# A graph layer on one core: cold edge lists read tile by tile, hot lists read from both ends of a block

## The chip, the cores and the metric

The kernel runs on one core of one Trainium2 chip. The metric is the device time of one launch in microseconds. The profiled execution is one launch recorded by the hardware profiler. The engines are PE (TensorE), DVE (VectorE), ACT (ScalarE), POOL (GpSimd) and SP (SyncE); each runs its instructions in program order and waits for others by semaphores.

## The reference

There are 6250 nodes with 256 features, and 200000 edges from `src` to `dst`, sorted by `dst`. `src` is uniform; `dst` is 6250 times the square of a uniform number, so that low node numbers are frequent destinations.

```python
xn = layernorm(x)
w  = sigmoid(relu(xn @ W1 + b1) @ W2 + b2)            # one number per node
num = segment_sum((xn * w)[dst], src); den = segment_sum(w[dst], src)
x = x + num / max(den, 1e-12) + mix(xn)                # mix: per-head linear attention over all nodes
f = layernorm(x)
# a router picks 2 of 6 experts; each expert is three 256x256 layers, the first two with relu
x = x + sum of the two experts' outputs, weighted
```

The part that the change touches is the pair of segment sums: for each node, the sum over its edges of the row `[xn * w, w]` of the other end.

## The kernel before, in words

The nodes are cut into 49 tiles of 128 (the last has 106), two tiles make a block of 256 (25 blocks), four tiles a group. A node's row `[xn * w, w, 1]` of 258 numbers is written to DRAM (`y_rows`) as three bf16 terms whose sum is the fp32 value, 774 numbers in all.

The edges are split by their place in the list, which is sorted by `dst`. Edges 0 to 65535 are the hot piece `b`: their destinations lie in the first 6 tiles. Edges 65536 to 131071 and 131072 to 196607 are the cold pieces `a` and `c`. The last 3392 are "few" edges; they are gathered 128 at a time (L501) and added to a table in DRAM by a scattering DMA (L522).

**Sorting.** Each piece is sorted on the chip by source node (`sort`, a bitonic network on DVE with turns on PE and copies back by ACT, L304 and L305), and written to DRAM as a list of packed keys (L346). `counts` finds where each block begins in a list: for each block border, one ACT activation (L354) takes the sign of `src` minus the border over the piece's 65536 edges and sums it; a matmul with ones adds the partitions, and `starts_of` turns the sums into `starts`.

**Cold edges.** For each block, `window_load` reads from each cold list a window of 23 x 128 keys that begins at the block's start. `cold_window` turns it and splits the keys into `dsts` and `srcs`. A cold step handles 128 edges: POOL gathers their 128 rows from `y_rows` by an indirect DMA (L851), DVE builds a 0/1 matrix `hot1` of edge against node (L859), and PE multiplies that matrix with the three terms of the gathered rows into the tile's sum `pu` (L876, three matmuls). The keys are in order of source, so the first tile of a block uses columns 0 to 11 of a window and the second columns 9 to 22; columns 9 to 11 hold edges of either, are gathered once and used in two steps. A block with both pieces has 52 steps and 46 gathers. Gathered rows lie in `GBUF` = 22 buffers. For the first 4 blocks (`LEAD`) piece `a` is done alone, then `c`, as `c` is sorted later. `Cold.step` is written so that gathers and matrices are issued `AHEAD` = 10 steps before their matmuls.

**Hot edges.** For each block a window of 23 x 128 keys is read from list `b`. In it the edges are in order of destination. `hot_counts` builds for each column `j` a matrix `to` (edge against source in the block, L1020) and, for each of 6 destination tiles `d` and each column that can hold edges into `d`, a matrix `fr` (edge against destination, L1022); their product, summed over columns (L1029), is a table of counts that is then multiplied with the hot rows, which stay in SBUF (L1048). `hot_range(blk, d)` gives the columns: the expected place of `d`'s edges, five standard deviations wide on both sides.

**The order of the work.** It is written out by a planner while the program is built. `run` interleaves generators (`Line`) by costs and due times that they yield; the first stretch interleaves the deviations of the first layernorm, the node rows (`node_rows`, `lines_y`), the sort of `a`, and the counts of `a` (`line_u[0]`). In the second, cold steps are paced by due times and run beside the few edges, the other two sorts and the head products; ACT's loads of the expert weights (L917 and after) reuse memory that the few edges' tiles held. From the first node term (L1073) on, class `Work` spends a credit after each cold step on node terms, hot sums and expert matmuls (L1188 bias, L1201, L1218). The credit per step is

```python
credit += max(0.0, (work.left - LAST) / (len(steps_c) - cold_edges.done + 1))
```

so that the cold steps spread evenly over the rest of the work, with `LAST` left for after the last of them. `ALL` is the planner's estimate of all that work. At the end the kernel sums the numbers of edges it has counted, and does all edges again by a slow path if the sum isn't 200000.

The functions as they stand before the change:

Of the kernel before, what the change touches and what calls it, by code (L numbers as in the profile page):

```python
# [27 lines left out]
GBUF = 22  # L28
# [10 lines left out]
class Piece:  # L39
# [4 lines left out]

    def __init__(self, name, start, row, used, cap, first, second):
        self.name, self.start, self.row, self.used, self.n = name, start, row, used, row * P
        self.cap, self.first, self.second = cap, first, second
# [3 lines left out]
def kernel(  # L51
# [61 lines left out]
    cold = [Piece("a", 65536, 512, P, 23, 12, 9), Piece("c", 131072, 512, P, 23, 12, 9)]  # L113
    hot = Piece("b", 0, 512, P, 23, 23, 0)
    pieces = cold + [hot]
    FEW = 196608
    NFEW = -(-(E - FEW) // P)
    HOT = 6
    NTHR = NBLK - 1
# [3 lines left out]
    def hot_range(blk, d):  # L123
        per = hot.n * min(BN, N - blk * BN) / N

        def bound(k, sign):
            at = min(1.0, E / hot.n * (P * k / N) ** 0.5) * per
            return at + sign * 5 * at**0.5

        lo = 0 if d == 0 else int(bound(d, -1) // P)  # L130
        hi = -int(-bound(d + 1, 1) // P)
        return max(0, lo), min(hot.cap, hi)
# [36 lines left out]
    nc.gpsimd.iota(thr, pattern=[[-BN, NTHR]], base=-BN, channel_multiplier=0, allow_small_or_imprecise_dtypes=True)  # L169
# [179 lines left out]
    def counts(i):  # L349

        p = pieces[i]
        junk = pool_of(p).tile([P, p.row], BF, name=f"junk_{p.name}")
        for b in range(NTHR):
            nc.scalar.activation(  # L354
                junk, raw[p.name][0], AF.Sign, bias=thr[:, b : b + 1], accum_out=cnts[:, i, b : b + 1]
            )
            yield 0, 60 + 1.1 * p.row

    starts = const.tile([P, len(pieces), NBLK], I32, name="starts")
    nc.vector.memset(starts, 0)  # L360

    def starts_of(i0):
# [394 lines left out]
    with tc.manual_schedule(engines=ORDERED):  # L757
# [4 lines left out]
        line_t.before = line_u[0].before = [line_l]  # L762
        first_lines = [line_l, line_d] + lines_y + [line_a, line_u[0], line_t]
# [17 lines left out]
    def window_keys(wt, name):  # L781
# [4 lines left out]
        keys = wn.tile([P, 2 * max(p.cap for p in pieces)], I32, name="keys")[:, :n]  # L786
# [3 lines left out]
    def cold_window(wt):  # L790

        keys, n = window_keys(wt, "a")
        dsts = wn.tile([P, 2 * cold[0].cap], I32, name="dsts")[:, :n]
        nc.vector.tensor_scalar(dsts, keys, (1 << LOW) - 1, None, op0=ALU.bitwise_and)
        srcs = wn.tile([P, 2 * cold[0].cap], I32, name="srcs")[:, :n]
# [9 lines left out]
    for i, (blk, ps) in enumerate(passes):  # L805
        first_step.append(len(steps_c))
        for half in range(min(SB, NTILE - blk * SB)):
            todo, c0 = [], 0
            for p in ps:
                a, b = (0, p.first) if half == 0 else (p.second, p.cap)  # L810
                todo += range(c0 + a, c0 + b)
                c0 += p.cap
            steps_c += [(i, half, j, j == todo[0], j == todo[-1]) for j in todo]

    class Cold:
# [9 lines left out]
        def load(self, i):  # L825

            while self.loaded <= min(i, len(passes) - 1):
# [3 lines left out]
                self.wt[self.loaded] = window_load(blk, ps, "a")  # L831
                self.loaded += 1

        def decode(self, i):
            self.load(i)
            dsts, srcs = cold_window(self.wt.pop(i))
            loc = wn.tile([P, 2 * cold[0].cap], FP, name="loc")[:, : srcs.shape[1]]
# [3 lines left out]
        def make(self):  # L841
# [7 lines left out]
            if (i, j) not in self.gts:  # L849
                gt = gp.tile([P, TERMS, W], BF, name="gt")  # L850
                nc.gpsimd.indirect_dma_start(  # L851
                    out=gt.rearrange("p k w -> p (k w)"),
                    out_offset=None,
                    in_=y_rows,
                    in_offset=bass.IndirectOffsetOnAxis(ap=dsts[:, j : j + 1], axis=0),
# [613 lines left out]
```

## Time and profile before

| | us |
|---|---|
| median of 3 runs | 2080.5 (2080.08 to 2090.24) |
| the profiled execution | 2081.42 |
| its span, first to last instruction | 2079.2 |

| engine | busy us | share | instructions |
|---|---|---|---|
| PE | 1800.9 | 87% | 10048 |
| DVE | 1328.0 | 64% | 5556 |
| ACT | 540.0 | 26% | 1100 |
| POOL | 1158.2 | 56% | 1195 |

How to read it: busy time counts an instruction from its start to its end, so that on POOL the time between two instructions is not counted, and PE's matmuls overlap, their ends being modelled. Shares of the whole span are averages over stages with different limits; the mean granted PE clock was 0.923 over the span and 1.00 from about 650 us on. The costliest groups of the page are the gathers (L851, x1128, 1083.3 us of POOL) and the cold matmuls (L876, x3816, which are 1272 steps of three).

### The profile page before, as it was taken

To read this page: it belongs to the slowest core of one execution; us is meant where nothing else is said; L and a number is where in the kernel's file an instruction comes from. 1 tells how busy PE (TensorE), PEld (TensorE's weight loads), DVE (VectorE), ACT (ScalarE), POOL (GpSimd) and SP (SyncE) were. 2 spreads that over 40 slices of the span, in tenths; PEclk is the share of its full clock that TensorE was granted. 3 is DMA by queue.
4 is the path that set the end of the run, shared out by engine and by line. 5 is a ranking of instruction groups with operands and counts; after the bars stand their busy time and mean duration, and the time that the engine had idled before them with its cause. 6 is when DMAs were issued, how large, how long until landed. Compare 5 with 4: busy or idle time off the path is not lost.

```text
span 2079.2 us, 31214 instructions
## 1 busy us (share of the span) xinstructions
PE 1800.9 (87%) x10048; PEld 1221.6 (59%) x10048; DVE 1328.0 (64%) x5556; ACT 540.0 (26%) x1100; POOL 1158.2 (56%) x1195
## 2 busy tenths in 40 slices
PE   0664499645588999999999999999999999999998
PEld 0343377423455676666766667666666666666556
DVE  8989778948786655557555656655656565565322
ACT  0675443100011212212121221212122122222332
POOL 0000267777556777676777767777776767760000
PEclk9765599867789999999999999999999999999999
DMA  9742356576546566565665656566565666650000
GB/s 256 233 152 83 88 136 163 126 203 192 151 128 174 150 165 182 148 185 149 174 178 155 194 144 177 163 163 189 159 182 157 164 180 164 194 140 18 1 11 14
DMA packets 158713, 311.04 MB, mean 150 GB/s; under 512 B 28859, under 2 KB 101728, under 8 KB 158544
## 3 DMA queue, kind: packets, MB, share of 16 engines
q0 software_dynamic: 77728, 232.33, 42.0%
q1 hardware_dynamic: 75460, 76.12, 11.7%
q10 hardware_dynamic: 5356, 0.55, 0.3%
q8 instruction: 80, 1.31, 0.3%
q14 instruction: 89, 0.73, 0.1%
HBM read 275.51 MB, written 33.40 MB: 149 GB/s over the span
## 4 chain that ended last, share of the span: by engine, by line
PE 69%; DVE 6%; DMA 1%; issue 1%; ACT 0%; DVEq 0%; SPq 0%; ACTq 0%
PE px L1201 24%; PE pu L876 18%; PE px L1218 12%; PE ph L1029 5%; PE ph L1048 5%; PE px L1188 1%; DVE fr L1022 1%; PE ph L1073 1%; PE px L1108 1%; DVE to L1020 1%; PE px L1101 0%; DVE hot L859 0%; PE px L1114 0%; DVE k_b L268 0%; DVE k_b L269 0%
## 5 line engine op out<-in xcount | busy, mean ns | idle before, releaser
L851 POOL DMA_INDIRECT gt<-y_rows,dsts x1128 | 1083.3, 960 | 675.4 <-DVE srcs L796 241.6
L876 PE MATMUL pu<-gt,hot 128*128 128x258 bf16 x3816 | 625.6, 282 | 3.6 <-DMA gt<-y_rows,dsts 3.0
L876 PEld LDWEIGHTS <-hot 128*128 128x128 bf16 x3816 | 381.7, 101 | 341.3 <-issue 258.6
L1022 DVE TENSOR_SCALAR fr<-count,rdl 128x128 bf16<-128x128 bf16 x1105 | 273.6, 270 | 95.8 <-PE ph L1029 94.9
L1210 ACT ACTIVATE h<-px,eb_t 128x512 f32<-128x512 f32 (+1 forms) x312 | 206.6, 662 | 429.2 <-PE px L1201 428.4
L859 DVE TENSOR_SCALAR hot<-count,loc 128x128 bf16<-128x128 bf16 x1272 | 292.3, 272 | 18.2 <-PE pu L876 17.2
L1201 PE MATMUL px<-fT,ew_t 128*128 128x512 f32 (+1 forms) x624 | 298.2, 573 | 0.3 <-ACT fT L1102 0.3
L1201 PE MATMUL px<-h,ew_t 128*128 128x512 f32 (+1 forms) x624 | 297.1, 570 | 0.0
L1218 PE MATMUL px<-ew_t,h 128*128 128x256 f32 (+1 forms) x1176 | 296.6, 380 | 0.0
L1227 DVE SCALAR_TENSOR_TENSOR acc<-px,gate,acc 128x256 f32<-128x256 f32 (+1 forms) x294 | 128.6, 478 | 196.6 <-PE px L1218 196.4
L1029 PE MATMUL ph<-to,fr 128*128 128x256 bf16 x1105 | 225.4, 280 | 19.6 <-DVE fr L1022 15.3
L1218 PEld LDWEIGHTS px<-ew_t,h 128*128 128x128 f32 (+1 forms) x1176 | 203.4, 190 | 25.0 <-issue 4.3
L1020 DVE TENSOR_SCALAR to<-count,hloc 128x256 bf16<-128x256 bf16 x562 | 170.5, 305 | 2.0 <-PE ph L1029 2.0
L1031 ACT CAST cn<-ph 128x256 bf16<-128x256 f32 x150 | 55.8, 372 | 361.4 <-PE ph L1029 355.5
L1029 PEld LDWEIGHTS <-fr 128*128 128x128 bf16 x1105 | 109.2, 99 | 65.9 <-DVE fr L1022 39.4
L1048 PE MATMUL ph<-yh,cn 128*128 128x258 bf16 x882 | 130.9, 273 | 0.0
L1058 DVE TENSOR_TENSOR cs<-ph,cs 128x258 f32<-128x258 f32 x49 | 20.9, 427 | 150.8 <-PE ph L1048 150.3
L1201 PEld LDWEIGHTS px<-fT,ew_t 128*128 128x128 f32 x624 | 96.3, 191 | 22.0 <-issue 14.9
L1201 PEld LDWEIGHTS px<-h,ew_t 128*128 128x128 f32 x624 | 95.8, 190 | 22.1 <-issue 17.6
L1048 PEld LDWEIGHTS <-cn 128*128 128x128 bf16 x882 | 85.7, 97 | 15.4 <-issue 2.3
L545 PE MATMUL turn<-ident,xs 128*128 128x128 f32 (+1 forms) x98 | 28.2, 407 | 74.9 <-ACT xs L536 72.3
L545 PEld LDWEIGHTS turn<-ident,xs 128*128 128x128 f32 (+1 forms) x98 | 17.0, 195 | 86.5 <-issue 49.2
(238 smaller groups left out, 1726.0 us busy)
## 6 DMA issues: line engine op xcount, KB each, us to landing
gt<-y_rows,dsts POOLq DMA_INDIRECT x1128
xs<-in_x_dram SPq DMA_DIRECT2D x24, 512.0 KB
y_rows<-ys SPq DMA_DIRECT2D x10, 774.0 KB
table<-zero SPq DMA_DIRECT2D x50, 129.0 KB
tb<-table SPq DMA_DIRECT2D x49, 129.0 KB
xnT_d<-xnT SPq DMA_DIRECT2D x12, 512.0 KB
xt<-xnT_d SPq DMA_DIRECT2D x12, 512.0 KB
u<-in_x_dram SPq DMA_DIRECT2D x12, 512.0 KB
```

The costliest lines, as they stand in the source:

```text
L851: nc.gpsimd.indirect_dma_start(out=gt.rearrange("p k w -> p (k w)"), out_offset=None, in_=y_rows, in_offset=bass.IndirectOffsetOnAxis(ap=d ...
L859: nc.vector.tensor_scalar(hot1, count[:, half * P : (half + 1) * P], loc[:, j : j + 1], None, op0=ALU.is_equal)
L876: nc.tensor.matmul(self.pu, hot1, gt[:, k], start=(start and k == 0), stop=(stop and k == TERMS - 1))
L1020: nc.vector.tensor_scalar(made[j1], count, loc[:, j1 : j1 + 1], None, op0=ALU.is_equal)
L1022: nc.vector.tensor_scalar(fr, count[:, :P], rdl[:, d1, j1 : j1 + 1], None, op0=ALU.is_equal)
L1029: nc.tensor.matmul(pa, matrices[i], made[j], start=(j == j0), stop=(j == j1 - 1))
L1031: nc.scalar.copy(cn[:, d], pa)
L1048: nc.tensor.matmul(pu[:, :W], cn[:, d, s * P : (s + 1) * P], yh[:, d, k], start=(d == 0 and k == 0), stop=(d == HOT - 1 and k == TERMS - 1),)
L1201: nc.tensor.matmul(ph[:, :rows], w[:, e, c, f * P : (f + 1) * P], ins[:, c, :rows], start=(c == 0), stop=(c == CB - 1),)
L1210: nc.scalar.activation(h[:, f, :rows], ph[:, :rows], AF.Relu, bias=bc)
L1218: nc.tensor.matmul(po[:r, j - j0], h2[:, c, j * P : j * P + r], ew_t[2][:, e, c, :], start=(c == 0), stop=(c == CB - 1),)
L1227: nc.vector.scalar_tensor_tensor(acc[:r, j, :], po[:r, j - j0], gate[:r, j, e : e + 1], acc[:r, j, :], op0=ALU.mult, op1=ALU.add)
```

## The change

Each tile, not each block, gets a start in the cold lists, and so its own windows of 12 x 128 keys; no column is shared by two tiles any more, and a tile takes 12 steps and 12 gathers per piece. For that the counts of `a` and `c` are taken at 48 borders instead of 24. Those of `a` are put first in the first stretch, due at 9 us of the planner's clock; before, they came after the loads. Those of `b` stay at 24 borders.

The hot window of a block is now read in two parts: 15 columns from the block's first edge on (`HEAD`), and 10 columns that end with its last edge (`TAIL`, at the next block's start minus 1280). Destination tiles 0 and 1 are taken from the head, tiles 2 to 5 from the tail, so that each range is measured from the nearer end. The two parts may overlap; an edge is counted in one of them alone, as its destination tile decides.

`GBUF` goes from 22 to 20, and the planner's estimate `ALL` has 37 hot matmuls per block instead of 45. Line numbers shift in the changed kernel (the cold matmul L876 becomes L905, the gather L851 becomes L880, the hot matmul L1029 becomes L1058).

```diff
-GBUF = 22
+GBUF = 20
...
-    cold = [Piece("a", 65536, 512, P, 23, 12, 9), Piece("c", 131072, 512, P, 23, 12, 9)]
-    hot = Piece("b", 0, 512, P, 23, 23, 0)
+    cold = [Piece("a", 65536, 512, 12), Piece("c", 131072, 512, 12)]
+
+    HEAD, TAIL = 15, 10
+    hot = Piece("b", 0, 512, HEAD + TAIL)
     pieces = cold + [hot]
+    NCOLD = sum(p.cap for p in cold)
...
-    NTHR = NBLK - 1
+    HEADS = 2
+    NTHR = NTILE - 1
...
     def hot_range(blk, d):
-        per = hot.n * min(BN, N - blk * BN) / N
+        per = min(BN, N - blk * BN) / N
+        head = d < HEADS
 
         def bound(k, sign):
-            at = min(1.0, E / hot.n * (P * k / N) ** 0.5) * per
+            below = min(E * (P * k / N) ** 0.5, hot.n)
+            at = (below if head else hot.n - below) * per
             return at + sign * 5 * at**0.5
 
-        lo = 0 if d == 0 else int(bound(d, -1) // P)
-        hi = -int(-bound(d + 1, 1) // P)
-        return max(0, lo), min(hot.cap, hi)
+        a, b = (d, d + 1) if head else (d + 1, d)
+        lo = max(0, int(bound(a, -1) // P))
+        hi = -int(-bound(b, 1) // P)
+        if head:
+            return lo, min(HEAD, hi)
+        return HEAD + max(0, TAIL - hi), HEAD + TAIL - lo
...
-    nc.gpsimd.iota(thr, pattern=[[-BN, NTHR]], base=-BN, channel_multiplier=0, allow_small_or_imprecise_dtypes=True)
+    nc.gpsimd.iota(thr, pattern=[[-P, NTHR]], base=-P, channel_multiplier=0, allow_small_or_imprecise_dtypes=True)
...
-        for b in range(NTHR):
+        for b in range(SB - 1 if p is hot else 0, NTHR, SB if p is hot else 1):
             nc.scalar.activation(
                 junk, raw[p.name][0], AF.Sign, bias=thr[:, b : b + 1], accum_out=cnts[:, i, b : b + 1]
             )
             yield 0, 60 + 1.1 * p.row
 
-    starts = const.tile([P, len(pieces), NBLK], I32, name="starts")
+    starts = const.tile([P, len(pieces), NTILE], I32, name="starts")
     nc.vector.memset(starts, 0)
+    nc.vector.memset(cnts, 0.0)
+
+    tails = const.tile([P, NBLK], I32, name="tails")
...
+        if pieces[i0] is hot:
+            nc.vector.memset(tails, hot.n - TAIL * P)
+            nc.vector.tensor_scalar(
+                tails[:, : NBLK - 1], starts[:, i0, SB::SB], float(-TAIL * P), 0.0, op0=ALU.add, op1=ALU.max
             )
...
-        line_t.before = line_u[0].before = [line_l]
-        first_lines = [line_l, line_d] + lines_y + [line_a, line_u[0], line_t]
+        line_t.before = [line_l]
+        line_u[0].due = 9000.0
+        first_lines = [line_u[0], line_l, line_d] + lines_y + [line_a, line_t]
...
-    def window_load(blk, ps, name):
+    def windows(ws, name):
 
-        wt = wn.tile([sum(p.cap for p in ps), P], FP, name=f"wt_{name}{len(ps)}")
+        wt = wn.tile([sum(n for _, _, n in ws), P], FP, name=f"wt_{name}{len(ws)}")
         c0 = 0
-        for p in ps:
-            at = nc.sync.value_load(starts[0:1, pieces.index(p), blk : blk + 1], min_val=0, max_val=p.n)
-            nc.sync.dma_start(
-                wt[c0 : c0 + p.cap], lists[p.name][bass.ds(at, p.cap * P)].rearrange("(j q) -> j q", q=P)
-            )
-            c0 += p.cap
+        for p, start, n in ws:
+            at = nc.sync.value_load(start, min_val=0, max_val=p.n)
+            nc.sync.dma_start(wt[c0 : c0 + n], lists[p.name][bass.ds(at, n * P)].rearrange("(j q) -> j q", q=P))
+            c0 += n
         return wt
+
+    def cold_load(blk, ps):
+        return windows(
+            [
+                (p, starts[0:1, pieces.index(p), t : t + 1], p.cap)
+                for t in range(blk * SB, min(NTILE, (blk + 1) * SB))
+                for p in ps
+            ],
+            "a",
+        )
+
+    def hot_load(blk):
+        i = pieces.index(hot)
+        return windows(
+            [(hot, starts[0:1, i, blk * SB : blk * SB + 1], HEAD), (hot, tails[0:1, blk : blk + 1], TAIL)], "b"
+        )
...
         for half in range(min(SB, NTILE - blk * SB)):
-            todo, c0 = [], 0
-            for p in ps:
-                a, b = (0, p.first) if half == 0 else (p.second, p.cap)
-                todo += range(c0 + a, c0 + b)
-                c0 += p.cap
+            n = sum(p.cap for p in ps)
+            todo = range(half * n, (half + 1) * n)
             steps_c += [(i, half, j, j == todo[0], j == todo[-1]) for j in todo]
...
-            if (i, j) not in self.gts:
-                gt = gp.tile([P, TERMS, W], BF, name="gt")
...
-                self.gts[i, j] = gt
+            gt = gp.tile([P, TERMS, W], BF, name="gt")
...
+            self.gts[self.made] = gt
...
-            hot1, gt = self.hot.pop(self.done), self.gts[i, j]
+            hot1, gt = self.hot.pop(self.done), self.gts.pop(self.done)
...
-    ALL = 1.1 * NTILE / GT * (64 * GT * P * F32NS + 2 * (45 * BFNS + 2 * HOT * TERMS * BFNS) + GT * 2 * P * F32NS)
+    ALL = 1.1 * NTILE / GT * (64 * GT * P * F32NS + 2 * (37 * BFNS + 2 * HOT * TERMS * BFNS) + GT * 2 * P * F32NS)
```

More of the change, by code (lines that the diff above doesn't have):

```diff
@@ L39, with __init__ @@
 class Piece:
-    def __init__(self, name, start, row, used, cap, first, second):
-        self.name, self.start, self.row, self.used, self.n = name, start, row, used, row * P
-        self.cap, self.first, self.second = cap, first, second
+    def __init__(self, name, start, row, cap):
+        self.name, self.start, self.row, self.n = name, start, row, row * P
+        self.cap = cap
 @with_exitstack
@@ L766 @@
         starts_of(0)
-    def window_load(blk, ps, name):
-        wt = wn.tile([sum(p.cap for p in ps), P], FP, name=f"wt_{name}{len(ps)}")
+    def windows(ws, name):
+        wt = wn.tile([sum(n for _, _, n in ws), P], FP, name=f"wt_{name}{len(ws)}")
         c0 = 0
-        for p in ps:
-            at = nc.sync.value_load(starts[0:1, pieces.index(p), blk : blk + 1], min_val=0, max_val=p.n)
-            nc.sync.dma_start(
-                wt[c0 : c0 + p.cap], lists[p.name][bass.ds(at, p.cap * P)].rearrange("(j q) -> j q", q=P)
-            )
-            c0 += p.cap
-        return wt
+        for p, start, n in ws:
+            at = nc.sync.value_load(start, min_val=0, max_val=p.n)
+            nc.sync.dma_start(wt[c0 : c0 + n], lists[p.name][bass.ds(at, n * P)].rearrange("(j q) -> j q", q=P))
+            c0 += n
+        return wt
+    def cold_load(blk, ps):
[11 more added lines that the diff above has]
+            [(hot, starts[0:1, i, blk * SB : blk * SB + 1], HEAD), (hot, tails[0:1, blk : blk + 1], TAIL)], "b"
+        )
     def window_keys(wt, name):
@@ L785, in window_keys @@
         nc.tensor.transpose(pT[:, :n], wt, ident[:n, :n])
-        keys = wn.tile([P, 2 * max(p.cap for p in pieces)], I32, name="keys")[:, :n]
+        keys = wn.tile([P, SB * NCOLD], I32, name="keys")[:, :n]
         nc.scalar.copy(keys.bitcast(FP), pT[:, :n])
@@ L792, in cold_window @@
         keys, n = window_keys(wt, "a")
-        dsts = wn.tile([P, 2 * cold[0].cap], I32, name="dsts")[:, :n]
+        dsts = wn.tile([P, SB * NCOLD], I32, name="dsts")[:, :n]
         nc.vector.tensor_scalar(dsts, keys, (1 << LOW) - 1, None, op0=ALU.bitwise_and)
-        srcs = wn.tile([P, 2 * cold[0].cap], I32, name="srcs")[:, :n]
+        srcs = wn.tile([P, SB * NCOLD], I32, name="srcs")[:, :n]
         nc.vector.tensor_scalar(
@@ L830, in load @@
                     self.sorted_to(p)
-                self.wt[self.loaded] = window_load(blk, ps, "a")
+                self.wt[self.loaded] = cold_load(blk, ps)
                 self.loaded += 1
@@ L836, in decode @@
             dsts, srcs = cold_window(self.wt.pop(i))
-            loc = wn.tile([P, 2 * cold[0].cap], FP, name="loc")[:, : srcs.shape[1]]
+            loc = wn.tile([P, SB * NCOLD], FP, name="loc")[:, : srcs.shape[1]]
             nc.vector.tensor_scalar(loc, srcs, float(-passes[i][0] * BN), None, op0=ALU.add)
@@ L848, in make @@
             dsts, loc = self.keys[i]
-            if (i, j) not in self.gts:
-                gt = gp.tile([P, TERMS, W], BF, name="gt")
[L851 to L855, printed above, removed]
-                )
-                self.gts[i, j] = gt
+            gt = gp.tile([P, TERMS, W], BF, name="gt")
+            nc.gpsimd.indirect_dma_start(
+                out=gt.rearrange("p k w -> p (k w)"),
+                out_offset=None,
+                in_=y_rows,
+                in_offset=bass.IndirectOffsetOnAxis(ap=dsts[:, j : j + 1], axis=0),
+            )
+            self.gts[self.made] = gt
             hot1 = hp1.tile([P, P], BF, name="hot1")
@@ L993, in hot_counts @@
         if blk + 1 < NBLK:
-            hot_wt[blk + 1] = window_load(blk + 1, [hot], "b")
+            hot_wt[blk + 1] = hot_load(blk + 1)
         hi = op1.tile([P, n], I32, name="hi")
@@ L1251, in __init__ @@
             self.time, self.landed = [0.0, 0.0], 0.0
-            hot_wt[0] = window_load(0, [hot], "b")
+            hot_wt[0] = hot_load(0)
         def next_load(self):
```

## The prediction

> **What bounds the kernel now.** I read the slices of the page first, then busy time in five stretches cut at events of the trace, then the POOL waits, then the time lines of POOL, PE and ACT around those events.
>
> Slices (40 of 52 us, busy tenths):
> ```profile
> PE   0664499645588999999999999999999999999998
> ...
> POOL 0000267777556777676777767777776767760000
> ```
> PE fills up only from about 650 us. POOL seems to have a quarter to spare throughout; it has not. The stretches end at the last scatter of the few edges (446.2), the first matmul of the node stage L1073 (550), the first L1188 (652.7) and the last cold matmul L876 (1885.5):
> ```profile
> core 0: us, PE busy (x) PEld busy (x) DVE busy (x) ACT busy (x) POOL busy (x), PEclk, DMA share, GB/s
> 0.00:446.20 446.20, 253.97 (x1341) 187.20 (x1341) 370.11 (x1171) 184.95 (x416) 149.40 (x140) 0.76 0.57 153
> 446.20:550.00 103.80, 50.49 (x275) 36.86 (x275) 76.39 (x264) 8.69 (x18) 73.20 (x74) 0.68 0.71 211
> 550.00:652.70 102.70, 84.02 (x537) 55.06 (x537) 84.93 (x442) 13.23 (x36) 59.01 (x62) 0.86 0.49 134
> 652.70:1885.50 1232.80, 1228.84 (x7146) 825.78 (x7147) 732.03 (x3440) 273.00 (x520) 876.59 (x920) 1.00 0.60 166
> 1885.50:2079.20 193.70, 0.00 (x0) 0.00 (x0) 0.99 0.04 11
> ```
> (The last line is that of L876 alone: no cold matmul is left, and 193.7 us of expert work follow.) The fourth stretch is the kernel: PE 99.7% busy, 920 gathers on POOL. A gather is busy 876.59/920 = 0.953 us, but back to back two are not 0.95 apart (POOL's time line; start, duration, idle before):
> ```profile
> 432.16 0.95 POOL L851 DMA_INDIRECT gt<-y_rows,dsts  x1 [0.30 <-issue]
> 433.41 0.95 POOL L851 DMA_INDIRECT gt<-y_rows,dsts  x1 [0.30 <-issue]
> ```
> and its waits in the fourth stretch (us, times, longest) show the same 0.3:
> ```profile
> POOL gt L851 <- issue: 124.7, 409, 0.3
> POOL gt L851 <- PE ph L1029: 92.0, 164, 4.9
> POOL gt L851 <- PE pu L876: 80.6, 215, 2.6
> ```
> 124.7/409 = 0.305 us of issue lie before each, so one gather costs POOL 0.953 + 0.305 = 1.258 us. 920 of them are 1157 us of the 1213 from 652.7 to the last gather at 1865.6. POOL is at 95% of its own limit; the other 56 us it waits for PE to free a gather buffer. PE bounds this stretch with POOL 5% behind it.
>
> **The change, part by part.** Counts are those of the two programs' instruction orders.
>
> (1) Cold steps. A full block takes 48 steps, each with a gather of its own, instead of 52 steps with 46 gathers: 1272 to 1176 steps, 1128 to 1176 gathers. A step's three matmuls take 0.34 us of PE:
> ```profile
> 1204.15 0.50 PE L876 MATMUL pu<-gt,hot 128*128 128x258 bf16 x3
> 1204.49 0.38 PE L1029 MATMUL ph<-to,fr 128*128 128x256 bf16 x2
> 1204.70 1.03 PE L1218 MATMUL px<-ew_t,h 128*128 128x256 f32 x4
> ```
> (0.34 from start to start; the bars overlap.) The two L1029 matmuls take 0.21, 0.107 each. In both programs 142 steps stand before the node stage, so all 96 fewer fall behind it: 15 in the third stretch, 81 in the fourth (1059 to 978).
>
> (2) Hot matrices. 1105 to 884: 20 fewer in the third stretch, 181 in the fourth (879 to 698), 20 in the tail. DVE builds 221 fewer `fr` (270 ns) and 50 more `to` (305 ns).
>
> Fourth stretch on PE: 1232.8 - 81 x 0.34 - 181 x 0.107 = 1232.8 - 27.5 - 19.4 = 1186 us.
> Fourth stretch on POOL: at its start PE has done 198 steps and POOL can be 20 buffers ahead, at 218, so 958 gathers remain: 958 x 1.258 = 1205 us, plus 3 for early waits while the buffers are still full, plus 3 for the last gather to land and be used: 1211 us. **So POOL becomes the bound**, and the stretch shrinks by 22 us, not by 47. PE then has 25 us idle, behind gathers not yet landed. GBUF 22 to 20 costs nothing while PE is the faster one; if PE is slower, POOL waits as it does now.
>
> Here two rules of the Trainium skill can be held against the rows. "DMA: Bandwidth & Descriptors", section "Latency and other measured facts", gives a DMA issued by GpSimd about 1 us of emission overhead. At 1.0 the 958 gathers would be 958 us, PE would stay the bound and the end come 25 us earlier than I say. The trace's pitch is 1.258, with the 0.30 us between two bars, and I take that. "SBUF - State Buffer", section "SBUF: two separate sides", speaks against this change: while VectorE runs an operation in a two-port mode, GpSimd can't write descriptors, and a DMA of 620 ns was seen to take 3100. DVE is 59% busy in the stretch (732/1232.8). By that rule even one gather in twenty so stretched would cost 48 x 2.5 = 120 us. The trace does not show it:
> ```profile
> L851 POOL DMA_INDIRECT gt<-y_rows,dsts x1128: 941/949/1500, 243.8 to 1865.6; - x188
> ```
> Minimum and median are 8 ns apart; I charge nothing.
>
> (3) Third stretch. DVE (84.9 of 102.7 us) and PE (84.0) both carry it. DVE loses 15 x 0.27 + 25 x 0.27 - 10 x 0.305 = 7.8 us, PE 15 x 0.34 + 20 x 0.107 = 7.2. I take -8; between 0 (latency alone) and -11.
>
> (4) The counts. 48 per cold piece instead of 24. One is a 0.72 us activation and a 0.19 us accumulator read, 0.85 apart. Piece a's move to the front of ACT: 29 ahead of `rstd_n` (13 + 29 x 0.85 = 38 us, before its 42.2: hidden), then 5, 3, 8 and 3 in the program order of the first node rows:
> ```profile
> 58.34 0.69 ACT L562 ACTIVATE hT<-ph,gb_t 128x512 f32<-128x512 f32 x1 [2.00 <-PE ph L556]
> ...
> 62.05 0.26 ACT L568 ACTIVATE w<-ph,gb_t 128x4 f32<-128x4 f32 x1
> ```
> The 5 fit into the 5.7 us before `xs`. The 3 delay the `xnT` copies at 53.1 and after by 2.6; the 8 run from 58.9 to 65.7, the two `hT` follow, then the 3: `w` at 70.8 instead of 62.05, +8.8. DVE reaches L582, which needs `w`, at 61.4 and holds piece a's sort behind it; DVE is 83% busy up to 446 us, so the delay stays. 24 fewer counts between 107 and 209 us give back some of DVE's small waits there (I count about 3). Net +6 at the first gather. Piece c's 24 more run from 245 us on in ACT's idle time (ACT is 35% busy there); up to 2 us of delay reach the `sm` copies that POOL's scatters wait for: +2.
>
> (5) POOL ahead of 446 us. The last scatter of the few edges stands behind 81 gathers instead of 74. It matters, as ACT's weight DMAs wait for it, and the sort's copy `t_b` for them:
> ```profile
> 448.10 0.40 ACTq L917 DMA_DIRECT2D rw_t<-in_L_ffn_router_w_dram  x1
> ...
> 449.73 0.59 ACT L305 COPY t_b<-turn 128x512 f32<-128x512 f32 x1 [26.47 <-DMA eb_t<-in_L_ffn_expert_b_dram]
> ```
> 7 x 1.258 = 8.8 us if POOL never waited; it waits some 12 us for `sm` around 271 to 289, ahead of which three of the seven stand, and 4 later. Between 0 and 8.8 I take 3.
>
> (6) Windows. 49 + 49 cold and 25 + 25 hot reads with a register load each, instead of 25 + 25 + 25, all on SP. Each is some 0.4 to 0.8 us of SP (two took 1.62), spread over 1600 us, and the keys are needed some 10 steps, 12 us, later. SP has such room: one wait of 0.8 us is all that the trace shows for a window read. If that cover were gone, 73 x 0.8 = 58 us could show. I charge 0. The clearing of `cnts` and the two operations for `tails` are some 0.2 us each (as `starts`, L368, 0.18), once: nothing.
>
> Sum: stretches one and two +6 +2 +3 = +11, third -8, fourth -22, tail 0 (20 hot matmuls less, 2 us, and as much expert work more): -19. The span goes from 2079.2 to 2060; with the 2.2 us around it, 2081.4 to 2062. The median of the runs is 0.9 below the profiled execution: 2061 to 2062. I forecast 2062.
>
> **The rivals.**
> *PE stays the bound.* If the gathers kept to less than 1186/978 = 1.213 us, the fourth stretch would be 1186 and the time about 2038. No stretch of the trace has gathers that close; against it stand all the rows above.
> *The buffer waits stay (slower).* POOL would be bound by its pitch and still wait, in bursts, for PE to free one of 20 buffers where there were 22. Place: L851 in the fourth stretch. Price: up to today's 56 us, giving 2062 + 53 = 2115. It decides from 18 us of waits on (an effective pitch of 1.277, no gain) and is over 0.5% slower from 30. For it: today's waits come in lumps of up to 4.9 us. Against it: a POOL that is the slower one empties its lead, and 20 buffers are 25 us of it.
> *The front costs more.* If (4) and (5) took their upper ends (+9, +3, +9) and the third stretch gave nothing, the front would lose 21, the fourth win 22: no change, 2081.
> *The windows don't hold their edges*, and the kernel computes all again, several times slower. The inputs exclude it: the fullest tile has 1431 edges of a piece, the window 1536.
>
> **How the numbers follow.** About 0.5%, 10 us, is what a measurement of this kernel can tell from no change. POOL as the bound with the small front cost: 0.58 (2050 to 2070). PE bound: 0.08 (2038). Front costs cancel it: 0.18 (2070 to 2090). Buffer waits or a longer pitch: 0.16 (2085 to 2115). Faster takes the first two less a little, 0.64; same 0.20; slower 0.16. Range: 2040 to 2090.
>
> **What would show it.** Right: in the fourth stretch gathers about 1.26 us apart with hardly a wait for L1029 or the cold matmul; cold matmuls that wait for DMA `gt`; PE busy down to some 98%. `w` near 71 us, the last scatter some 11 us later. Wrong: POOL waits of over 20 us in that stretch, a median gather of over 0.96 us, PE still above 99.5%, or the first L1188 later than 665.

## The result, and the profile after

| | median us | runs (lowest to highest) |
|---|---|---|
| before | 2081.45 | 9 (2079.95 to 2090.24) |
| after | 2074.97 | 9 (2071.71 to 2076.93) |

The ratio is 0.995, with a 95% interval of 0.9932 to 0.9968: the changed kernel is 6.5 us faster, where 19 had been forecast. The profiled execution of after took 2076.93 us, with a span of 2075.1.

The runs of the experiments fell on several chips. On one of them the kernel before takes 2081.7 us, much as in the table; on two others it takes 2351.5 and 2348.3. The first is called the quick chip here, the other two the slow chips; whether the chip itself makes the difference, or something else about these runs, is not known. Every ratio below is against the kernel before on the same chip. The prediction is about the quick chip, and so is everything up to the last part of the experiments.

The slices of the page of after:
```profile
PE   0564389635588999999999999999999999999997
...
POOL 0000167877646777777777777777777777770000
```
POOL's row used to change between 6 and 7. From slice 14 on it is a flat row of sevens: POOL works at one constant rate until it has nothing left. The digit is only 7 because the 0.30 us before each gather do not count as busy.

The stretches of after, cut at the same events as before (last scatter, first node matmul, first bias matmul of the experts, last cold matmul), and then the third and the last stretch of before:
```profile
core 0: us, PE busy (x) PEld busy (x) DVE busy (x) ACT busy (x) POOL busy (x), PEclk, DMA share, GB/s
0.00:454.00 454.00, 250.52 (x1343) 185.19 (x1343) 370.24 (x1173) 226.21 (x513) 157.05 (x147) 0.76 0.57 153
454.00:546.20 92.20, 51.94 (x262) 37.01 (x263) 70.21 (x242) 8.70 (x18) 70.99 (x72) 0.64 0.73 214
546.20:659.70 113.50, 81.00 (x489) 50.73 (x487) 86.67 (x435) 14.38 (x39) 64.48 (x67) 0.80 0.53 145
659.70:1872.80 1213.10, 1190.73 (x6712) 784.99 (x6713) 688.84 (x3218) 271.71 (x517) 916.04 (x960) 0.99 0.64 175
1872.80:2075.10 202.30, 187.03 (x739) 117.64 (x736) 62.17 (x226) 59.71 (x110) 0.00 (x0) 0.96 0.04 11
```
```profile
535.00:652.70 117.70, 85.38 (x550) 56.11 (x548) 91.81 (x465) 13.23 (x36) 67.27 (x71) 0.83 0.52 143
1885.10:2079.20 194.10, 184.00 (x755) 117.08 (x752) 64.58 (x241) 60.28 (x111) 0.00 (x0) 0.99 0.04 11
```
Here "first node matmul" is the first instance of its line, at 535.0 us before; the prediction's cut at 550 was the second burst of that line. Both are cut at the first one in this table:

| stretch, us | before | after | change | forecast |
|---|---|---|---|---|
| start to first node matmul | 535.0 | 546.2 | +11.2 | +11 |
| to the first bias matmul (third) | 117.7 | 113.5 | -4.2 | -8 |
| to the last cold matmul (fourth) | 1232.4 | 1213.1 | -19.3 | -22 |
| to the end (tail) | 194.1 | 202.3 | +8.2 | 0 |
| sum | 2079.2 | 2075.1 | -4.1 | -19 |

In the fourth stretch PE now idles 22.4 us (1213.10 less 1190.73). POOL's waits there (us, times, longest) and PE's largest wait:
```profile
POOL gt L880 <- issue: 125.3, 411, 0.3
POOL gt L880 <- PE pu L905: 72.5, 234, 1.1
POOL gt L880 <- PE ph L1058: 31.7, 104, 0.3
```
```profile
PE pu L905 <- DMA gt<-y_rows,dsts: 19.6, 24, 2.4
```
Before, the waits for PE were up to 4.9 us long. Now nearly all are 0.3, the issue time that precedes every gather whatever its releaser is called: the waits beyond it add up to 0.4 us in the stretch, against 57.0 before. In exchange the cold matmul waits 24 times for its gathered rows. The two engines have changed roles. POOL's last two gathers, still at a steady 1.26 us (start, duration, idle before):
```profile
1866.38 0.96 POOL L880 DMA_INDIRECT gt<-y_rows,dsts  x1 [0.30 <-PE px L1230]
1867.64 0.94 POOL L880 DMA_INDIRECT gt<-y_rows,dsts  x1 [0.30 <-issue]
```
The 959 gathers that start in the stretch have a mean pitch (start to start) of 1.2605 us: 958 x 1.2605 = 1207.5 us, 0.4 before the first and 5.2 from the last gather's start to the last cold matmul give 1213.1.

### The profile page after: what moved, and what is told of

The parts are those of the page before. It is cut to its first block, busy times and chain, and to the rows that moved or that the text cites. A ratio compares the mean times of both kernels' runs of the same rounds, so it can differ in the third digit from the quotient of the medians.

```text
span 2075.1 us, 30397 instructions
## 1 busy us (share of the span) xinstructions
PE 1761.2 (85%) x9539; PEld 1175.5 (57%) x9539; DVE 1278.1 (62%) x5292; ACT 580.7 (28%) x1197; POOL 1208.6 (58%) x1243
## 3 DMA queue, kind: packets, MB, share of 16 engines
q8 instruction: 77, 1.26, 0.3%
## 4 chain that ended last, share of the span: by engine, by line
PE 62%; DVE 8%; DMA 6%; issue 2%; POOL 1%; ACT 1%; SPq 0%; ACTq 0%; DVEq 0%; POOLq 0%
PE px L1230 23%; PE pu L905 15%; PE px L1247 11%; DMA gt<-y_rows,dsts 5%; PE ph L1077 5%; PE ph L1058 4%; DVE fr L1051 1%; PE px L1217 1%; DVE to L1049 1%; PE px L1137 1%; PE ph L1102 1%; DVE k_b L277 1%; DVE k_b L278 1%; POOL gt L880 1%; DVE hot L888 1%
## 5 line engine op out<-in xcount | busy, mean ns | idle before, releaser
L880 POOL DMA_INDIRECT gt<-y_rows,dsts x1176 | 1133.0, 963 | 634.9 <-DVE srcs L829 247.5
L905 PE MATMUL pu<-gt,hot 128*128 128x258 bf16 x3528 | 593.2, 285 | 28.6 <-DMA gt<-y_rows,dsts 27.4
L905 PEld LDWEIGHTS <-hot 128*128 128x128 bf16 x3528 | 355.4, 102 | 370.3 <-issue 292.8
L1230 PE MATMUL px<-fT,ew_t 128*128 128x512 f32 (+1 forms) x624 | 303.9, 583 | 0.0
L1230 PE MATMUL px<-h,ew_t 128*128 128x512 f32 (+1 forms) x624 | 296.1, 569 | 0.0
L888 DVE TENSOR_SCALAR hot<-count,loc 128x128 bf16<-128x128 bf16 x1176 | 271.1, 271 | 20.6 <-PE pu L905 20.1
L1051 DVE TENSOR_SCALAR fr<-count,rdl 128x128 bf16<-128x128 bf16 x884 | 226.6, 271 | 40.7 <-PE ph L1058 40.1
L1058 PE MATMUL ph<-to,fr 128*128 128x256 bf16 x884 | 183.7, 284 | 21.0 <-DVE fr L1051 15.6
L1049 DVE TENSOR_SCALAR to<-count,hloc 128x256 bf16<-128x256 bf16 x612 | 183.7, 302 | 7.4 <-PE ph L1058 7.2
L1058 PEld LDWEIGHTS <-fr 128*128 128x128 bf16 x884 | 87.7, 99 | 63.8 <-DVE fr L1051 42.1
L1230 PEld LDWEIGHTS px<-fT,ew_t 128*128 128x128 f32 x624 | 98.4, 195 | 23.4 <-issue 16.5
L1230 PEld LDWEIGHTS px<-h,ew_t 128*128 128x128 f32 x624 | 96.0, 190 | 22.6 <-issue 18.2
```

The lines of the kernel that those rows point to most:

```text
L880: nc.gpsimd.indirect_dma_start(out=gt.rearrange("p k w -> p (k w)"), out_offset=None, in_=y_rows, in_offset=bass.IndirectOffsetOnAxis(ap=d ...
L888: nc.vector.tensor_scalar(hot1, count[:, half * P : (half + 1) * P], loc[:, j : j + 1], None, op0=ALU.is_equal)
L905: nc.tensor.matmul(self.pu, hot1, gt[:, k], start=(start and k == 0), stop=(stop and k == TERMS - 1))
L1049: nc.vector.tensor_scalar(made[j1], count, loc[:, j1 : j1 + 1], None, op0=ALU.is_equal)
L1051: nc.vector.tensor_scalar(fr, count[:, :P], rdl[:, d1, j1 : j1 + 1], None, op0=ALU.is_equal)
L1058: nc.tensor.matmul(pa, matrices[i], made[j], start=(j == j0), stop=(j == j1 - 1))
```

## The experiments

Three theories were set against each other. **POOL binds**: after the change the gathers' pitch sets the fourth stretch, so fewer PE instructions are worth nothing there and fewer gathers are. **PE binds**: both kernels are bound by PE, and the gain should be the sum of its parts. **The gather costs its pitch everywhere**: 48 more of them add their whole 1.26 us each, and the change could only lose.

**Hot part alone.** The kernel before, with only the hot windows in two parts:
```diff
-    hot = Piece("b", 0, 512, P, 23, 23, 0)
+    HEAD, TAIL = 15, 10
+    hot = Piece("b", 0, 512, P, HEAD + TAIL, 23, 0)
...
-            hot_wt[blk + 1] = window_load(blk + 1, [hot], "b")
+            hot_wt[blk + 1] = hot_load(blk + 1)
```


> Hot windows in two parts and shifted tails, gathers shared as before (1128). On the chip where the kernel before takes about 2081 us: POOL-bound theory: 884 instead of 1105 hot matmuls free PE while POOL has slack (its 918 gathers of the fourth stretch at 1.258 us are 1155 us), so the fourth stretch falls from 1232 to about 1205 and the whole to 2050 to 2066. Rival (hot matmuls lie beside other waits and are worth nothing): 2072 to 2083. Where the kernel before takes about 2351 us, a ratio near 0.998 again.

Measured: 2067.18 us (2065.85 to 2069.66), ratio 0.9919 (0.9902 to 0.9936). The fourth stretch fell from 1232.4 to 1216.4, and not to 1205; the total is 1 above the range, and below the rival's. (The prediction's term for it, 181 matmuls at 0.107 us, is 19.4 us and gives 1213. The rest is near the loss of clock: the trace has four periods of half clock in the stretch instead of two, each of 3.4 us.) The fourth stretch, and POOL's waits for PE in it:
```profile
655.10:1871.50 1216.40, 1213.60 (x6955) 809.33 (x6956) 704.32 (x3300) 270.92 (x518) 871.68 (x917) 0.99 0.60 168
```
```profile
POOL gt L874 <- PE pu L899: 110.4, 253, 4.5
POOL gt L874 <- PE ph L1052: 48.0, 108, 3.1
```
PE is still full (2.8 us idle), and POOL still has waits of up to 4.5 us, together 48 us beyond issue time. PE is the bound of this version.

**Cold part alone.** The changed kernel, with the hot edges read in one window of 23 columns as before:
```diff
-    HEAD, TAIL = 15, 10
-    hot = Piece("b", 0, 512, HEAD + TAIL)
+    hot = Piece("b", 0, 512, 23)
```


> Each tile reads its own stretches of the cold lists (1176 gathers and steps), hot edges in one window of 23 columns as before. On the chip where the kernel before takes about 2081 us: POOL-bound theory: 96 fewer steps of 0.34 us on PE (-33 us, some 26 of them in the fourth stretch) against 40 more gathers in that stretch; POOL and PE are then about level at 1205 to 1210 us, and the front costs +11: 2070 to 2082. Rival (a gather more costs its whole pitch of 1.26 us on the path, 48 of them 60 us): 2110 to 2140. Where the kernel before takes about 2351 us, a ratio near 1.009 again.

Measured: 2072.9 us (2072.22 to 2073.64), ratio 0.995 (0.9933 to 0.9966), within the POOL theory's range. The same two views:
```profile
655.20:1868.20 1213.00, 1203.91 (x6902) 801.62 (x6903) 717.82 (x3361) 272.89 (x519) 915.17 (x963) 1.00 0.63 176
```
```profile
POOL gt L865 <- PE pu L890: 61.8, 203, 0.3
POOL gt L865 <- PE ph L1043: 42.0, 138, 0.3
```
No POOL wait is longer than 0.3 us any more, while PE has 9.1 us idle. The four versions together are the clearest test (gathers are those of the whole program):

| fourth stretch, us (whole, us) | one hot window | two hot parts |
|---|---|---|
| shared columns (1128 gathers) | 1232.4 (2081.5) | 1216.4 (2067.2) |
| own columns (1176 gathers) | 1213.0 (2072.9) | 1213.1 (2075.0) |

The hot part takes 190 matmuls out of the stretch in the lower row (6902 less 6712) and moves it by 0.1 us. The same part in the upper row takes out 188 and wins 16. Once each tile has its own gathers, POOL's time is the floor and the hot part has nothing to win. If PE bound all four, the parts' gains in the whole (14.5 and 8.8) would add up to 23; together they give 6.5.

**Fewer gathers, the same PE work.** The changed kernel with
```diff
-            gt = gp.tile([P, TERMS, W], BF, name="gt")
-            nc.gpsimd.indirect_dma_start(
...
+            if j % 12 == 11:
+                gt = self.last_gt
+            else:
+                gt = self.last_gt = gp.tile([P, TERMS, W], BF, name="gt")
+                nc.gpsimd.indirect_dma_start(
```


> The changed kernel, but every twelfth step multiplies with the rows that the step before it gathered: 98 of 1176 gathers are left out (so part of the sums is of other rows), PE's work is the same. On the chip where the kernel before takes about 2081 us: POOL-bound theory: about 80 gathers fewer in the fourth stretch are 100 us off POOL, so PE becomes the bound, and only PE's 22.7 us of idle time in that stretch can be won: 2043 to 2058. Rival (PE bounds the changed kernel too): 2070 to 2078. If a gather costs its whole pitch of 1.26 us or more: 1950 or less. Where the kernel before takes about 2351 us, a ratio near 0.96 again.

This kernel leaves out a part of the sums. Measured: 2035.95 us (2033.32 to 2039.69), ratio 0.9767 (0.9749 to 0.9786): 39 us below the changed kernel and 7 below the range expected. Its fourth stretch:
```profile
650.10:1836.50 1186.40, 1183.48 (x6711) 784.32 (x6712) 691.53 (x3218) 271.75 (x517) 834.40 (x878) 0.99 0.59 166
```
The matmuls are those of the changed kernel (6711 and 6712), yet the stretch is 26.7 us shorter, and PE is full again: its idle time falls from 22.4 to 2.9 us, and the other 7 us are busy time, about half of it from two periods of half clock less. This refutes PE as the bound of the changed kernel. Eighty-two gathers less are 103 us of POOL, of which only 27 come through: then PE's own time ends the stretch, at 1186.4, where the prediction's step-by-step sum for PE had 1186. The gathers therefore don't cost their pitch everywhere either. Most of the 7 us that were not expected lie ahead of the node stage: only 76 gathers stand before the last scatter instead of 81, the scatter starts at 447.7 instead of 454.0, and the node matmul 7.0 earlier. Five gathers at 1.26 us are 6.3: in this version each gather in that place is worth its whole pitch.

**Can PE's idle time be used?** The kernel holds back 150 us of dense work for the time after the last gather. The changed kernel with
```diff
-LAST = 150000.0
+LAST = 120000.0
```


> The changed kernel with LAST = 120000 instead of 150000, which lets 30 us more of dense work go ahead of the last gathers. POOL-bound theory: PE idles 22.7 us in the fourth stretch waiting for gathered rows, and that idle time can be filled with dense work that now lies in the tail: the tail falls by about 30 us and the stretch grows by what does not fit, 8 us: about 22 us less than the changed kernel, so 2053 (2048 to 2062) where it takes 2075. Rival (dense work goes ahead only as it comes due, and PE's idle time lies in stretches too short for it): within 5 us of the changed kernel, 2070 to 2080.

Measured: 2045.62 us (2045.02 to 2048.53), ratio 0.9822 (0.9804 to 0.984): 29 us below the changed kernel, 2 better than the range, and 1.8% faster than the kernel before. Its fourth stretch and tail:
```profile
656.70:1876.50 1219.80, 1215.00 (x6825) 801.75 (x6826) 701.09 (x3261) 276.61 (x529) 913.79 (x960) 0.99 0.63 175
1876.50:2043.20 166.70, 153.75 (x625) 98.25 (x623) 49.82 (x182) 52.22 (x98) 0.00 (x0) 0.97 0.03 8
```
The tail loses 35.6 us and the stretch takes only 6.7 of them back. PE's idle time there falls from 22.4 to 4.8 us. PE's busy time in the whole program falls too, from 1761.2 to 1750.6, with the same 9539 matmuls; after 660 us the granted clock falls to half in four periods of 3.4 us instead of seven, and about half of such a period is lost, so that three periods make some 5 us of the 10.6 (an estimate from these figures). The rest of the 10.6 was not followed.

**The same kernels on a slow chip.** The changed kernel itself, then the parts:

> The changed kernel once more, for its stages: the front (last scatter at 454, first bias matmul of the experts at 660) and the fourth stretch (1213 us) should come out within 2 us. The tail after the last cold matmul was 202 us, 8 more than before; if that is the program it is 202 again, if it is chance of the run (half-clock windows, the closing of the program) it lies between 195 and 203. Median 2072 to 2077.

Measured: 2371.9 us against 2351.51, ratio 1.01 (1.0064 to 1.0136). On this chip the change makes the kernel slower. The tail is 200.7 us, near the 202 that was expected if the program makes it and not chance.

> The kernel before with the hot part alone: windows in two parts and 884 hot matmuls instead of 1105; cold windows, counts, buffers as before. Theory (gathers 1.26 us apart are the limit as soon as PE gets faster than that): before, PE is the slower one in the fourth stretch (1233 us against 920 x 1.258 = 1157 of POOL), so 181 hot matmuls less at 0.107 are 19 us of time, and POOL still has room (1163 against 1213). With 4 to 6 us in the third stretch and nothing lost ahead: about 2057 (2050 to 2066), clearly faster than the whole change. Rival (the hot matmuls are not on the path, the gain of the change is that of the cold part): 2072 or more.

Measured: 2345.16, ratio 0.9976 (0.9959 to 0.9993).

> The changed kernel with the hot part undone (one window of 23 columns from the block's first edge, 1105 hot matmuls). Theory: the front loses its 11 us as in the changed kernel, the fourth stretch is bound by POOL's 958 gathers at 1.26 = 1208 us with PE at 1232 - 27 = 1205 beside it, so that it ends as in the changed kernel or a few us later: 2074 to 2082. Rival (both parts add up on PE): the changed kernel plus 21 to 24 us, 2096 to 2099.

Measured: 2369.7, ratio 1.0087 (1.0059 to 1.0115).

> The changed kernel without the gather of every twelfth step: that step multiplies the rows of the step before it, so 98 of 1176 gathers are left out and all matmuls stay. Theory: POOL's share of the fourth stretch falls to 878 x 1.26 = 1106 us, PE is the bound again at about 1188, 25 us shorter than the 1213 of the changed kernel; ahead of it the last scatter stands behind 6 gathers less, 0 to 7 us: 2043 to 2052. Rival (PE's idle time comes from the latency of gathers or from elsewhere, not from POOL's pace): 2070 or more.

Measured: 2255.2, ratio 0.9599 (0.9563 to 0.9635). The numbers expected were meant for the quick chip; of these runs only the ratios can be used, and they differ in more than size. The changed kernel's fourth stretch on this chip, POOL's waits in it, and its gathers (shortest/median/longest ns):
```profile
704.20:2164.30 1460.10, 1280.45 (x6712) 810.05 (x6713) 688.22 (x3218) 268.34 (x517) 912.67 (x960) 0.94 0.53 146
```
```profile
POOL gt L880 <- issue: 189.9, 611, 0.9
POOL gt L880 <- PE pu L905: 154.3, 165, 2.1
POOL gt L880 <- remote: 50.0, 37, 2.2
```
```profile
L880 POOL DMA_INDIRECT gt<-y_rows,dsts x1176: 940/947/1542, 250.6 to 2143.2; - x196
```
The gathers are as short as on the quick chip (median 947 against 949 ns), and so is the start of the program: the first gather is at 250.6 us, against 249.7. But POOL waits 235 us beyond issue time, in many pieces of one to two us under all kinds of names, "remote" among them (a releaser that the profile can't place), and the mean pitch is 1.502 us. PE idles 180 us, and the same matmuls keep it busy 90 us longer, at a granted clock of 0.94. PE's largest waits in this stretch:
```profile
PE ph L1058 <- issue: 30.7, 30, 4.1
PE px L1217 <- issue: 18.8, 4, 6.7
PE ph L1058 <- ACT cn L1060: 17.0, 8, 4.2
```
So POOL's pace is not what PE waits for there. No wait of the stretch is put down to gathered rows, and the last gather starts 21.1 us before the last cold matmul, against 5.2 on the quick chip: POOL is well ahead. What the trace does show is that the engines stand still together. At one place (start, duration, idle before) none of them is busy for 1.0 us, and then they go on within half a microsecond:
```profile
1448.24 0.94 POOL L880 DMA_INDIRECT gt<-y_rows,dsts  x1 [0.79 <-remote]
1450.22 0.65 ACT L1060 CAST cn<-ph 128x256 bf16<-128x256 f32 x2 [1.84 <-remote]
1450.31 0.87 DVE L1256 SCALAR_TENSOR_TENSOR acc<-px,gate,acc 128x256 f32<-128x256 f32 x2 [4.51 <-remote]
1450.42 0.94 POOL L880 DMA_INDIRECT gt<-y_rows,dsts  x1 [1.24 <-remote]
```
Added up over the stretch, PE, DVE, ACT and POOL are idle at once for 50 us, in pieces of up to 1.7 us; on the quick chip it is 0.9 us. What stops them was not found. The packets of the gathers' DMA queue are not slower: between 700 and 1800 us they take 183 ns on average, against 184.

The versions on the slow chips, the third of them from a run that follows below:

| slow chips | gathers in the fourth stretch | PE matmuls | its length, us | mean pitch, us |
|---|---|---|---|---|
| every twelfth left out | 877 | 6711 | 1366.2 | 1.531 |
| hot part alone | 917 | 6954 | 1444.2 | 1.552 |
| kernel before with LAST = 120000 | 919 | 7271 | 1460.8 | 1.569 |
| changed kernel | 959 | 6712 | 1460.1 | 1.502 |
| cold part alone | 960 | 6902 | 1473.4 | 1.515 |
| own gather for each step | 1038 | 7143 | 1578.9 | 1.503 |

Here both counts show in the length. With the same matmuls, 82 gathers less take away 93.9 us, 1.15 each; with 1.15 taken off for one gather more, 190 matmuls add 12.1, 0.064 each. The third and the fourth row are equally long, with 40 gathers more and 559 matmuls less in the fourth. By these two figures the change would make the stretch 18 us longer (the 40 gathers that it adds on the quick chip are 46 us, the 431 matmuls that it takes out there are 28): an estimate, which fits the sign, 2371.9 against 2351.5. Neither bound of the prediction explains why a gather costs so much where PE does not wait for it.

**More gathers, the same PE work**, also on a slow chip (before: 2348.26). The kernel before, without sharing:
```diff
-            if (i, j) not in self.gts:
+            if True:
```


> The kernel before, but each of the 52 steps of a pair of tiles has its own gather: the 6 shared columns are gathered twice, 1272 gathers instead of 1128, PE's 1272 steps unchanged. POOL-bound theory: about 117 gathers more in the fourth stretch make some 1035 x 1.258 = 1302 us of POOL against PE's 1232 there, so the stretch grows by 70 us, and 27 more gathers before it cost up to 30: 2150 to 2180. Rival (gathers run beside PE's work, and what matters is PE's steps): 2081 to 2090. On the chip where the kernel before takes about 2351 us: more than 1.05 against less than 1.02.

Measured: 2480.36 us, ratio 1.0577 (1.0545 to 1.0608), the number that the POOL theory has for that chip. PE's matmuls are those of the kernel before (7143 in the fourth stretch), so there sharing the columns is worth 5.8%. It does not show that POOL's pace binds: PE's cold matmuls wait 2.4 us in all for gathered rows. On the quick chip this version was not run. Its fourth stretch:
```profile
698.30:2277.20 1578.90, 1356.92 (x7143) 850.18 (x7143) 730.40 (x3441) 269.40 (x519) 986.48 (x1039) 0.94 0.52 145
```

**The control that didn't control.** LAST = 120000 in the kernel before was to show whether that edit is worth something where PE is full:

> The kernel before with LAST = 120000 instead of 150000, the control for the changed kernel with the same edit (2045.6 us, 29 less than the changed kernel). Theory that PE bounds the kernel before: PE idles only 4.3 us in its fourth stretch, so dense work moved ahead of the last gather finds no idle time and only lengthens the stretch by what the tail loses: 2077 to 2083, against 2081. Rival (the edit is worth 20 us or more whatever bounds the stretch, so that it says nothing of POOL): 2050 to 2062. On the chip where the kernel before takes about 2351 us: ratio 0.997 to 1.002 against 0.99 or less.

Measured, on a slow chip: 2326.51 us, ratio 0.9916 (0.9885 to 0.9947), between the two expectations and nearer to the rival. But on that chip PE idles 126 us in this kernel's fourth stretch even so (1460.8 less 1334.8), so there is idle time to fill, and the run says nothing of the quick chip. It was not run there. On this chip the edit is worth 21.8 us in the kernel before and 22.8 in the version of the changed kernel that follows (2365.8 to 2343.0), so that here, by these two pairs, its gain does not depend on the change.

**The counts.** Two versions of the changed kernel with piece a's counts in two lots:
```diff
-            yield 0, 60 + 1.1 * p.row
+            yield 0, (60 + 1.1 * p.row) if i or b != 28 else 45000.0
```


> The changed kernel with piece a's counts paused for 45 us of ACT's work after the 29th, the rest unchanged. Theory that the front's loss is from ACT's 23 added counts ahead of the first `w`: w back to 62 to 65 us, the first gather at 244 to 246 us, the whole 5 to 6 us less than the changed kernel: 2069 (2066 to 2072). Rival (the front's loss comes from POOL's own queue, more gathers ahead of the last scatter): w falls, but the node terms start as late as before, and the time stays at 2073 to 2077.

> The changed kernel with LAST = 120000 and with the counts of piece a paused for 45 us of ACT's work after the 29th, so that 19 of 48 come after the norms of the first group instead of before them. Theory that the late first `w` (70.6 us against 62.05) carries through to the first gather and the node terms: 6 us less than with LAST alone (2045.6): 2040 (2035 to 2043). Rival (ACT's counts are only moved, and hold up later norms or piece c as much): 2044 to 2050.

Measured, on the second slow chip: 2365.77 us, ratio 1.0069 (1.0022 to 1.0115), and 2343.0 us, ratio 0.9975 (0.9953 to 0.9997). The first interval overlaps that of the changed kernel on the other slow chip (1.0064 to 1.0136), so the times don't tell the two theories apart. The trace of the first does tell one thing:
```profile
62.10 0.26 ACT L586 ACTIVATE w<-ph,gb_t 128x4 f32<-128x4 f32 x1
```
`w` is back at 62.1 us, as before the change, but the first gather stays at 251.0 (changed kernel: 250.6). The second has `w` at 63.1 and its first gather at 248.8. The trace also says why: the delay has only moved, as the rival had it. The 19 paused counts run between 97.1 and 128.2 us, and in that time DVE, and piece a's sort on it, waits for copies and for a later `w` that come behind them on ACT (waits between 97 and 149 us; before, none of this time is over 2.0):
```profile
DVE k_a L277 <- ACT k_a L314: 4.4, 1, 4.4
DVE t_a L262 <- ACT t_a L314: 4.0, 1, 4.0
DVE ys L600 <- ACT w L586: 3.3, 1, 3.3
```
The sorted list is written at 230.9 us, as late as in the changed kernel on the other slow chip (230.2; the kernel before with LAST = 120000: 222.9). Of the versions run that compute all of the sums, LAST = 120000 alone remains the best on the quick chip; splitting the counts was not run there.

## Why the prediction was right, and where it was off

The time of 2075 lies in the stated range of 2040 to 2090, but outside the 2050 to 2070 that the main case was given. The range takes in the rival of no change too, so that the time alone decides little between them; the stretches and the experiments do. The mechanism was right; two terms of the sum were mis-sized.

1. *POOL becomes the bound, the fourth stretch shrinks by 22 and not by 47.* Shown. The stretch shrank by 19.3, and ended at 1213.1 against 1211. Both bounds came out as worked out: POOL's in the changed kernel (pitch 1.260 against 1.258, 959 gathers against 958), PE's once gathers were left out (1186.4 against 1186). The sign of what was expected in the profile also held: no waits for PE, and cold matmuls that wait for `gt`. One sum of the prediction is off without consequence: the pitch under which PE would have stayed the bound divides by 978 steps where 958 gathers belong, and is (1186 - 6)/958 = 1.23 us and not 1.213.

2. *The third stretch gives 8.* It gave 4.2, all of it PE's busy time (85.38 to 81.00); PE's idle time in it is unchanged (32.3 and 32.5 us). PE has 61 matmuls less there, near the 65 forecast, but they came out at 0.07 us each and not at 0.107 and 0.113: the granted clock of the stretch fell from 0.83 to 0.80, and 3% of 81 us are 2.4 us (an estimate). DVE lost 5.1 us of work instead of 7.8. Direction right, size half.

3. *The front loses 11.* It lost 11.2, and its terms held in size: `w` at 70.59 us (70.8 forecast), the first gather 5.9 later (6 forecast), the last scatter 9.3 later (6 + 2 + 3 forecast, with the 2 only to show in what follows it). The chain behind the 6 held too. DVE's wait for the first `w`, before and after (us, times, longest), grows by as much as `w` is late:
```profile
DVE yh L582 <- ACT w L568: 1.0, 1, 1.0
DVE yh L600 <- ACT w L586: 9.1, 1, 9.1
```
Piece a's sort, next on DVE, goes on 8.5 us later there. It wins back 2.6 of them (3 forecast), and its list is written at 229.7 instead of 223.7. POOL's part can be checked as well: between the first gather and the last scatter it has seven gathers more, 9.1 us more busy and 2.1 of issue, but waits 7.9 us less (15.9 to 8.0), net +3.4 where 3 was taken.

4. *The tail is unchanged.* This is the term that was mis-sized, and the largest miss: it grew by 8.2 us. Two things make it up. From the last cold matmul to the start of PE's last one it takes 190.8 us instead of 186.3. PE has 16 matmuls less there, but is busy 3.0 us longer: the granted clock of the tail is 0.96 instead of 0.99, from two periods of half clock of 3.4 us each, from 1903.0 and 1981.5 us on, where before has none (the matmuls of L1230 start 0.85 us apart in the first of them, and 0.43 after it). The rest is idle time, with 1.3 us of waits for DVE's `fr` that before did not have. And the program takes 11.5 us to close after that, instead of 7.8: the trace shows POOL's sequencer 7.9 us in its last semaphore step and drain (1.70 and 6.18), against 3.0 (0.74 and 2.27). These two durations are the same in every profile of a program with as many gathers, on the quick and on the slow chips. The prediction counted instructions for the tail and left out the program's end, which no row of busy instructions shows.

5. *Windows, clearing and tails cost nothing; GBUF costs nothing.* The windows do come onto the chain that ended last, at one place, after the write of the sorted hot list. The chain there (start, duration, what), before and then after:
```profile
538.09 3.81 DMA list_b<-k_b
541.92 0.34 SPq L736
542.36 5.03 DMA xt<-list_b
...
550.05 2.08 PE ph L1073 x8
```
```profile
549.02 3.74 DMA list_b<-k_b
...
556.85 0.53 SPq L793
...
557.88 1.94 DMA wt_b<-list_b
...
560.61 2.07 PE ph L1102 x8
```
From the start of that write to the node matmuls it takes 11.96 us before and 11.59 after: SP's register loads and window reads (L793, L794) take the place of a read of 5 us, and the path is no longer for it. In the fourth stretch POOL's waits beyond issue are 0.4 us, and PE has no wait for a window.

6. *VectorE does not slow the gathers.* DVE is 57% busy in the stretch after the change (688.84/1213.10) and the gathers are at 943/949/1536 ns.

By the profiles the forecast hoped for 14.9 us more than came: 8.2 of them are the tail, 3.8 the third stretch and 2.7 the fourth. Of the rivals, "the front costs more" (2081) was nearest to the time, but not for its reason: the front cost what was forecast, and the loss came at the end. The prediction had no case for the slow chips. There the change costs 1.0%, its cold part alone 0.9%, and the hot part alone wins 0.2%; the traces do not show POOL as the bound, and the cause is open.

## What to carry to other kernels

When two engines are within 5% of one another, work out what each would take alone, pitch times count with the issue gap included: the gain ends where the second engine becomes the bound, and idle time that the first then has can be filled with other work (here by letting dense work start earlier: 29 us, of which some 18 are idle time filled; how much of it the kernel before would win on the quick chip was not run). Check a change of this kind on its parts as well as whole: the hot part alone was worth more, 14.5 us, than both together, 6.5. And a small gain by which one engine's load is traded for another's may not carry to another chip: the ratio was 0.995 on one and 1.010 on another.

## What the runs showed of the hardware that was not expected

- Chips differ: the kernel before takes 2081 us on one and 2350 on two others, at the same median duration of a gather (946 to 949 ns in all versions). In the changed kernel's fourth stretch all four engines are idle at once for 50 us on a slow chip and for 0.9 on the quick one. Up to its first gather it takes the same time on both, to 1 us.
- The close of the program costs 7.4 to 12.2 us from the start of PE's last matmul on, and it depends on the program, not on the run: POOL's last semaphore step and drain take 3.0 us with 1128 gathers, 7.9 with 1176, 6.9 with 1272 and 8.7 with 1078. It does not grow with the number of gathers; its rule is open.
- The granted clock falls to half for 3.4 us at a time, and how often depends on the kernel: on the quick chip, from 660 us to the close, twice in the kernel before, four times in the cold part alone, with every twelfth gather left out and with LAST = 120000, five times in the hot part alone, seven times in the changed kernel. It does not simply follow PE's idle time: the hot part alone has PE as full as the kernel before in the fourth stretch (2.8 against 4.0 us idle).
